# A state space layer on one core: when the experts' weights are loaded and split, and where its side work stands in the order of work

## The chip, the core and the metric

The kernel runs on one core of one Trainium2 chip. The core has TensorE (PE: matrix products, and transposes by a product with the identity), VectorE (DVE), ScalarE (ACT), GpSimd (POOL) and SyncE (SP, which here only issues transfers), 16 DMA engines, and two on-chip memories, SBUF and PSUM. Each engine takes its instructions in one order and waits, where it must, on semaphores that another engine or a transfer raises. The metric is the device time of one execution of the whole kernel in microseconds (us).

## The reference

The model has four layers: a state space layer, a layer of eight experts, a linear attention with a feed-forward part, and two local attention layers. The change touches only the first two, which the kernel computes together. On x of 4 x 1024 tokens of 256 values:

```python
x = x + _L0_attn_ref(_layernorm(x), ...)     # state space layer
x = x + _L0_ffn_ref(_layernorm(x), ...)      # experts
...
def _L0_attn_ref(x, W_in, conv_w, conv_b, W_xproj, W_dt, b_dt, A_log, D, W_out):
    xz = einsum('bld,ed->ble', x, W_in)
    u, z = split(xz, 2)                      # 512 channels each
    uc = silu(conv1d(u, conv_w, padding=1) + conv_b)     # 3 taps along the tokens
    dtp, Bm, Cm = split(uc @ W_xproj.T)      # 64, 16 and 16 wide
    dt = softplus(dtp @ W_dt.T + b_dt)
    A = -exp(A_log)                          # 16 states
    def step(h, inp):
        u_t, dt_t, B_t, C_t = inp
        h = exp(dt_t[:, None, :] * A[None, :, None]) * h + B_t[:, :, None] * u_t[:, None, :]
        return h, einsum('bn,bnh->bh', C_t, h)
    y = scan(step) + D * uc
    return x + (y * silu(z)) @ W_out.T

def _L0_ffn_ref(x, router_w, router_b, expert_w, expert_b):
    probs = softmax(x @ router_w.T + router_b)           # 8 experts
    top1, weights = argmax(probs), max(probs)
    y = (x @ expert_w[top1].T + expert_b[top1])
    return y * weights
```

## The kernel before

The method `mamba` computes both layers. Its 4096 tokens are cut into 16 sub-sequences `s` of 256 tokens, four to a batch row. The channels lie on the partitions (512 channels are four groups of 128), the tokens along them, and the 16 states are worked through one after the other. So there are 16 x 16 = 256 steps `k`, each one sub-sequence and one state `n`.

A step of the main loop does, in the order in which it is written:

- POOL keeps the last column of an earlier state (`keep`, tile `carry`), adds the carried start to the next one (`take`), and multiplies `uc` by a row of B for the step after the next: `product`, `hs<-uc,bn`, 128 x 1024, four `hs` buffers in all.
- ACT computes the decays exp(dt A) of half of the channels of the next step: `decays`, `da<-dt,a`, in PSUM, three buffers.
- DVE runs the recurrence in place over half of the channels, twice a step: `scan`, `hs<-da,hs`. "Scan 17" below means the second scan of step 8 of a sub-sequence, counted from 0.
- PE turns the result to tokens first, eight transposes: `tokens_first`, `ph<-ident,hs`, two `ph` buffers in PSUM. The step before's `ph` is weighted by C: for the states 0 to 5 by DVE into one sum (`acc<-ph,ct`), for the states 6 to 15 by ACT into tiles of their own (`term<-ph,ct`).

All else is side work, written as Python generators whose pieces end at `yield`:

- `features(s)`: loads a sub-sequence (`xr`), normalizes it (`st`, `mv`, `xn`), turns it (`xth`, `xtl`: a value split into a high and a low part, so that three products make one of higher precision).
- `channels(s)`: products with W_in (`pz`, `pu`), convolution and silu (`uc`, `sz`).
- `sizes(s)`: B, C and dt. `px` and `xd`; then B goes to DRAM (`bd`) and is read back to all partitions (`bn`); `ct`; two `pd` products, each with a group of ACT operations behind it; then a logarithm on ACT, which takes a table load on either side (`ACT_TABLE_LOAD`), and `dt`. With `first`, the next sub-sequence's decays can begin.
- `finish(s)`: sums the terms on PE (`py`), multiplies by the gate, the product with W_out (`po`), and adds it to `xr` on DVE (`xr<-xr,po`).
- `experts(s)`: norm, router (`pl`), choice (`cw`), bias (`pb`), and for every pair of experts six PE products into `pe`, weighted and added on DVE (`xr<-pe,cw,xr`, two of them); then `xr` is stored (`xs`).
- `expert_weights()`: runs once, in the first sub-sequence. It splits the router's weights `w_r` and the experts' weights `w_e`, eight parts of 128 x 512. For a part it loads `raw` (two buffers, shared by all of these loads and held until their splits are done), then ACT casts `raw` to `w_eh` and POOL subtracts, `w_el<-raw,w_eh`.

Where the pieces stand is given by lists of places. A step has three places (`PER`): 3k after the first scan and its output, 3k+1 after the second, 3k+2 after the transposes; a sub-sequence has 48, and a place below 0 or above 47 lies in the sub-sequence before or after. `side(place)` runs the next piece of each generator listed there, and within the loop every engine keeps the order in which its instructions were written (`nc.hold`); the order of transfers isn't held. `PSUM` tiles of all side work share three buffers (`tag="w"`), so a piece also waits for the piece three tiles earlier to be read.

All instructions are recorded in one helper (line 98), so that profile rows are told apart by their tiles. In the prologue, before the loop, `features(0)`, `features(1)`, `channels(0)`, `sizes(0)` and `features(2)` are run whole, then the first two `bn` loads are issued, and the loop is entered with two products and two decays. For sub-sequence 0 `sizes` does its `dt` sums on DVE instead of POOL (`dt<-dt,e`).

Of the kernel before, what the change touches and what calls it, by code (L numbers as in the profile page):

```python
# [17 lines left out]
P = 128  # L18
D = 256
# [15 lines left out]
NE = 8  # L35
# [38 lines left out]
def parts(width):  # L74
    return [slice(o, min(o + 512, width)) for o in range(0, width, 512)]


def run(steps):

    while True:  # L80
        try:
            next(steps)
        except StopIteration as end:
            return end.value
# [40 lines left out]
class Kernel:  # L125
# [145 lines left out]
    def mamba(self, xs):  # L271

        tc, ins = self.tc, self.ins
        nc = self.nc
# [4 lines left out]
        with ExitStack() as es:  # L279
            def pool(name, bufs, **kw):  # L280
                return es.enter_context(tc.tile_pool(name=name, bufs=bufs, **kw))

            early = pool("m_a", 1)
# [23 lines left out]
            for at in parts(2 * CH):  # L307
                for k in range(2):
                    raw = self.raw(early, ins["w_in"][k * P : (k + 1) * P, at])
# [20 lines left out]
            def expert_weights():  # L330
                w_e = Split(
                    wp.tile([P, 2, NE * D], F32R, name="w_eh"),
                    wp.tile([P, 2, NE * D], F32R, name="w_el"),
                )
                w_r = Split(
                    wp.tile([P, 2, NE], F32R, name="w_rh"), wp.tile([P, 2, NE], F32R, name="w_rl")
                )
                for k in range(2):
                    raw = self.raw(early, ins["w_r"][k * P : (k + 1) * P, :])
                    self.split(w_r[:, k, :], raw)  # L340
                yield
                for at in parts(NE * D):
                    for k in range(2):
                        raw = self.raw(early, ins["w_e"][k * P : (k + 1) * P, at])
                        self.split(w_e[:, k, at], raw, nc.gpsimd)
                        yield

                eb = wp.tile([2 * NE, 2, D], F32, name="eb")
                nc.gpsimd.memset(eb, 0.0)
                for t in range(2):  # L350
                    nc.scalar.dma_start(eb[t * NE : (t + 1) * NE, t, :], ins["e_b"])
                rank = wp.tile([P, NE], F32, name="rank")
                for e in range(NE):
                    nc.gpsimd.memset(rank[:, e : e + 1], float(NE - e))
                ew.update({"e": w_e, "r": w_r, "eb": eb, "rank": rank})
                ew["rb"] = self.row(wp, "router_b", NE)
                yield
# [51 lines left out]
            def channels(s):  # L409

                xt = st[s]["xt"]
                uc = mid.tile([P, NC, T], F32, name="uc", bufs=3)
                sz = mid.tile([P, NC, T], F32, name="sz", bufs=3)

                def gate(q):
                    pz = ps.tile([P, 2, T], F32, tag="w", name="pz")
                    for j in range(2):
                        o = CH + (2 * q + j) * P
                        self.mm3(
                            pz[:, j, :],  # L420
                            [(w_in[:, k, o : o + P], xt[:, k, 1 : T + 1]) for k in range(2)],
                        )
                    nc.scalar.copy(sz[:, 2 * q : 2 * q + 2, :], pz)

                def conv(c):
                    pu = ps.tile([P, T + 2], F32, tag="w", name="pu")
                    self.mm3(pu, [(w_in[:, k, c * P : (c + 1) * P], xt[:, k, :]) for k in range(2)])
                    nc.scalar.activation(
                        uc[:, c, :], pu[:, 1 : T + 1], AF.Identity,
                        bias=self.v("conv_b", c), scale=self.v("conv", NC + c),  # L430
                    )
                    return c, pu

                def neighbours(c, pu):
                    u = uc[:, c, :]
                    for j in (0, 2):
                        nc.vector.scalar_tensor_tensor(
                            u, pu[:, j : j + T], self.v("conv", j * NC + c), u, ALU.mult, ALU.add
                        )

                if s == 0:

                    for c in range(NC):
                        neighbours(*conv(c))
                    nc.scalar.activation(uc, uc, AF.Silu)
                    gate(0)
                    gate(1)
                    nc.scalar.activation(sz, sz, AF.Silu)
                else:
                    gate(0)  # L450
                    yield
                    gate(1)
                    one = conv(0)
                    yield
                    neighbours(*one)
                    one, two = conv(1), conv(2)
                    yield
                    neighbours(*one)
                    neighbours(*two)
                    one = conv(3)  # L460
                    yield
                    neighbours(*one)
                    yield

                    nc.scalar.activation(uc, uc, AF.Silu)
                    nc.scalar.activation(sz, sz, AF.Silu)
                st[s].update({"uc": uc, "sz": sz})
                yield
# [76 lines left out]
            def taken(s, o):  # L545

                first, at = st[s]["first"], slice(o, o + NS // 2)
                nc.gpsimd.tensor_tensor(
                    first[:, at, :], first[:, at, :], st[s - 1]["carry"][:, at, :], ALU.mult
                )  # L550
# [61 lines left out]
            def output(k, t):  # L612

                s, n = divmod(k, NS)
                ph, w = st[s]["ph", n, t], st[s]["ct"][:, t, n : n + 1]
                if n == 0 and t == 0:
                    st[s]["terms"] = [mid.tile([P, 2, CH], F32, name="acc", bufs=2)]
                terms = st[s]["terms"]
                acc = terms[0][:, t, :]
                if n in LATER:  # L620
                    if t == 0:
                        terms.append(mid.tile([P, 2, CH], F32, name=f"term{n}"))
                    nc.scalar.activation(terms[-1][:, t, :], ph, AF.Copy, scale=w)
                elif n == 0:
                    nc.vector.tensor_scalar(acc, ph, w, None, ALU.mult)
                else:
                    nc.vector.scalar_tensor_tensor(acc, ph, w, acc, ALU.mult, ALU.add)
# [35 lines left out]
            def experts(s):  # L663
# [83 lines left out]

            TAKEN = (19,)  # L750
            FINISH = (4, 7, 7, 13, 15, 17, 22, 25)
            CHANNELS = (-9, -5, -2, 0, 5, 8)
            SIZES = (10, 13, 16, 22, 26, 31, 37)
            FEATURES = (4, 14, 26, 30, 33, 34, 40)
            EXPERTS = (
                33, 33, 37, 40, 42, 43, 47, 51, 53, 53, 58, 62, 66, 75, 77, 81,
                82, 85, 87, 89, 95,
            )
            PER = 3
            plan = [[] for _ in range(PER * NSUB * NS)]  # L760

# [3 lines left out]
            def at(steps, step, places, plan=plan):  # L765
                for i in places:
                    plan[max(0, PER * step * NS + i)].append(steps)

            rest = []
            at(expert_weights(), 0, [PER * i + 1 for i in range(10)])  # L770
            for s in range(NSUB):
                last = s == NSUB - 1
                if s % SEQ:
                    at(iter([lambda s=s: taken(s, NS // 2)]), s, TAKEN)
                if s > 0:
                    at(finish(s - 1), s, FINISH)
                if not last:
                    at(channels(s + 1), s, CHANNELS)
                    at(sizes(s + 1), s, SIZES)
                if s + 3 < NSUB:  # L780
                    at(features(s + 3), s, FEATURES)
                if s > 0:
                    e = experts(s - 1)
                    if last:
                        at(e, s, [PER * i + 1 for i in range(9, NS) for _ in range(2)], later)
                        rest.append(e)
                    elif s + 1 == NSUB - 1:
                        at(e, s, EXPERTS[:7], later)
                        at(e, s + 1, [PER * i + 1 for i in range(14)], later)
                    else:  # L790
# [2 lines left out]
            run(features(0))  # L793
            run(features(1))
            run(channels(0))
            run(sizes(0))
            run(features(2))
            inputs(0)
# [13 lines left out]
            for k in range(K):  # L812
# [12 lines left out]
                if k:  # L825
                    output(k - 1, 0)
                side(PER * k)
                scan(k, 1)
# [1192 lines left out]
```

## Time and profile before

| what | us |
|---|---|
| median of the runs (3356.81 to 3365.26) | 3365.12 |
| the profiled execution's own time | 3363.27 |
| its span | 3361.6 |
| PE busy in the span | 3117.1 |
| DVE busy | 2558.7 |
| ACT busy | 2078.3 |
| POOL busy | 1932.1 |

The mean TensorE clock granted over the span was 0.963 of full speed. The span starts with a prologue up to the first scan at 43.80; the sub-sequences follow up to about 1084, then linear attention and the local attention layers. Times of rows are from the span's start. In a row of instructions the columns are the start, the duration, the engine, the line, the operation, the tile written and the tiles read, their shapes and the count; in square brackets is the engine's idle time before it, and what it waited for. A row of several instructions ("x3") tells the time from the first's start to the last's end. The page's shares are averages over stages with different limits: what bounds the first third isn't to be read from the whole.

### The profile page before, as it was taken

Reading aid. Unit: us, or ns where it says so; the run is one execution under the profiler, and the core shown is the slowest. Engines: PE = TensorE matmul, PEld = TensorE weight load, DVE = VectorE, ACT = ScalarE, POOL = GpSimd, SP = SyncE. Lnnn points to the kernel's source line nnn. Section 1 sums busy time; section 2 is a strip of 40 time slices with the busy share of each in tenths; the row PEclk is TensorE's granted clock in tenths of the full one; section 3 lists DMA queues with packets and bytes.
Section 4 is the critical chain, followed back from the end, with each engine's and each line's share of the span. In section 5 each row is a group of like instructions: output and inputs, shape, how many; then the busy total and the mean of one; then the engine's idle time right before and its main releaser. Section 6 shows DMA issues by size and latency. Waiting matters only on the chain.

```text
span 3361.6 us, 60088 instructions
## 1 busy us (share of the span) xinstructions
PE 3117.1 (93%) x22000; PEld 2670.1 (79%) x22000; DVE 2558.7 (76%) x5684; ACT 2078.3 (62%) x4194; POOL 1932.1 (57%) x2285
## 2 busy tenths in 40 slices
PE   5788899898888899999999999899999999999998
PEld 4677777777777688888888888688888888888886
DVE  6799999999997766666776757677777677767763
ACT  7888887888884323443434343666666776667664
POOL 5988988898885401101110114766677766767671
PEclk7799999999998999999999999899999999999998
DMA  2011111111110300000000011201111111111111
GB/s 93 32 45 39 39 51 39 39 39 45 36 41 30 99 8 4 14 7 14 20 10 10 20 39 50 79 26 43 45 51 50 51 47 55 43 47 39 46 35 35
DMA packets 83974, 130.62 MB, mean 39 GB/s; under 512 B 10080, under 2 KB 58016, under 8 KB 83680
## 3 DMA queue, kind: packets, MB, share of 16 engines
q1 hardware_dynamic: 81216, 124.68, 11.6%
q8 instruction: 175, 2.87, 0.4%
q10 hardware_dynamic: 2320, 1.57, 0.2%
q14 instruction: 119, 0.97, 0.1%
q0 software_dynamic: 144, 0.52, 0.0%
HBM read 99.21 MB, written 27.53 MB: 38 GB/s over the span
## 4 chain that ended last, share of the span: by engine, by line
PE 58%; DVE 18%; ACT 12%; POOL 6%; issue 4%; DMA 2%; POOLq 0%; SPq 0%; ACTq 0%; DVEq 0%
PE pw L98 10%; PE pq L98 10%; PE po L98 8%; PE pa L98 7%; DVE hs L98 7%; PE pt L98 7%; ACT L98 3%; PE pf L98 3%; PE pp L98 3%; PE pv L98 2%; ACT gl L98 2%; DVE acc L98 2%; POOL hs L98 2%; PE pe L98 2%; PE ph L98 2%
## 5 line engine op out<-in xcount | busy, mean ns | idle before, releaser
L98 DVE TENSOR_TENSOR_SCAN hs<-da,hs 128x512 f32<-128x512 f32 x512 | 609.2, 1209 | 20.9 <-ACT da L98 10.8
L98 POOL TENSOR_TENSOR hs<-uc,bn 128x1024 f32<-128x1024 f32 x256 | 608.7, 2378 | 26.8 <-PE ph L98 22.5
L98 PE MATMUL ph<-ident,hs 128*128 128x128 f32 x2048 | 333.8, 299 | 126.8 <-ACT term L98 52.0
L98 PEld LDWEIGHTS ph<-ident,hs 128*128 128x128 f32 x2048 | 249.8, 152 | 208.5 <-DVE hs L98 71.8
L98 ACT ACTIVATE da<-dt,a 128x510 f32<-128x510 f32 x512 | 342.8, 686 | 91.9 <-DVE hs L98 85.2
L98 POOL MEMSET va<- 128x8 f32 x64 | 7.3, 117 | 575.2 <-PE pk L98 458.2
L98 POOL TENSOR_TENSOR u<-u,ro 128x512 f32<-128x512 f32 x128 | 175.5, 1371 | 246.9 <-DVE ro L98 201.2
L98 ACT ACTIVATE sm<-sm,mx 128x256 f32<-128x256 f32 (+1 forms) x512 | 248.5, 488 | 97.8 <-DVE mx L98 96.8
L98 PE MATMUL pq<-wqkvh,yt 128*128 128x512 f32 x768 | 287.8, 416 | 0.7 <-ACT yt L98 0.7
L98 POOL TENSOR_SCALAR sm<-sm,sums 128x256 f32<-128x256 f32 (+1 forms) x512 | 237.2, 481 | 83.0 <-DVE sums L98 77.7
L98 ACT ACTIVATE term<-ph,ct 128x512 f32<-128x512 f32 x320 | 207.6, 681 | 45.1 <-PE ph L98 45.0
L98 ACT ACT_TABLE_LOAD x146 | 187.3, 1283 | 59.7 <-DVE gl L98 31.9
L98 DVE CUSTOM_DVE_ANT_0 sm<-pp,band 128x256 f32<-128x256 f32 (+1 forms) x512 | 177.8, 403 | 42.5 <-PE pp L98 42.1
L98 POOL TENSOR_TENSOR ss<-ss,power 128x16 f32<-128x16 f32 x64 | 187.7, 2932 | 5.3
L98 ACT ACTIVATE e<-pq 128x512 f32<-128x512 f32 x128 | 75.9, 597 | 182.7 <-PE pq L98 170.1
L98 PEld LDWEIGHTS pq<-wqkvh,yt 128*128 128x128 f32 x768 | 144.9, 189 | 38.3 <-issue 9.8
L98 ACT ACTIVATE sq<-pq 128x512 f32<-128x512 f32 x128 | 76.6, 599 | 142.8 <-DVE ro L98 106.6
L98 PE MATMUL py<-ident,term 128*128 128x128 f32 x1280 | 159.5, 276 | 0.0
L98 PE MATMUL pq<-wqkvl,yt 128*128 128x512 f32 x384 | 152.4, 397 | 0.0
L98 PE MATMUL pa<-fh,w1h 128*128 128x512 f32 x320 | 134.2, 420 | 19.1 <-ACT v L98 15.7
L98 PEld LDWEIGHTS py<-ident,term 128*128 128x128 f32 x1280 | 147.1, 144 | 0.1
L98 PE MATMUL po<-va,am 128*128 128x65 f32 x1024 | 146.4, 260 | 0.0
(323 smaller groups left out, 10256.3 us busy)
## 6 DMA issues: line engine op xcount, KB each, us to landing
bn<-bd SPq DMA_DIRECT2D x64, 512.0 KB
tab<-tab SPq DMA_DIRECT2D x64, 128.0 KB
line<-yg SPq DMA_DIRECT2D x64, 128.0 KB
hn<-line SPq DMA_DIRECT2D x64, 128.0 KB
xr<-in_x SPq DMA_DIRECT2D x16, 256.0 KB
xs<-xr SPq DMA_DIRECT2D x16, 256.0 KB
hn<-xs SPq DMA_DIRECT2D x16, 256.0 KB
ls<-hn SPq DMA_DIRECT2D x16, 256.0 KB
```

What stands on the lines that cost most here:

```text
L98: now = f(*args, **kw)
```

## The change

Two things are changed in `mamba`. `expert_weights()` is started by hand in the prologue, between `channels(0)` and `sizes(0)`: there it splits `w_r` and issues the loads of the first two parts of `w_e`. Each later piece splits one part, and then issues the load of the part after the next. Its pieces have a list of places of their own, `WEIGHTS`: three at place 1, then 4, 7, 10, 13, 17 and 25, where before there were ten at 1, 4, 7 and so on up to 28. And all the other lists of places are replaced. The same operations are done as before.

```diff
                 for k in range(2):
                     raw = self.raw(early, ins["w_r"][k * P : (k + 1) * P, :])
                     self.split(w_r[:, k, :], raw)
-                yield
-                for at in parts(NE * D):
-                    for k in range(2):
-                        raw = self.raw(early, ins["w_e"][k * P : (k + 1) * P, at])
-                        self.split(w_e[:, k, at], raw, nc.gpsimd)
-                        yield
+
+                order = [(k, at) for at in parts(NE * D) for k in range(2)]
+                raws = [self.raw(early, ins["w_e"][k * P : (k + 1) * P, at]) for k, at in order[:2]]
+                yield
+                for i, (k, at) in enumerate(order):
+                    self.split(w_e[:, k, at], raws[i], nc.gpsimd)
+                    if i + 2 < len(order):
+                        k, at = order[i + 2]
+                        raws.append(self.raw(early, ins["w_e"][k * P : (k + 1) * P, at]))
+                    yield
...
-            TAKEN = (19,)
-            FINISH = (4, 7, 7, 13, 15, 17, 22, 25)
-            CHANNELS = (-9, -5, -2, 0, 5, 8)
-            SIZES = (10, 13, 16, 22, 26, 31, 37)
-            FEATURES = (4, 14, 26, 30, 33, 34, 40)
+            TAKEN = (20,)
+            FINISH = (4, 7, 7, 10, 14, 17, 21, 25)
+            CHANNELS = (-11, -5, -2, 1, 6, 9)
+            SIZES = (10, 13, 18, 22, 25, 31, 43)
+            FEATURES = (7, 11, 25, 30, 33, 34, 38)
             EXPERTS = (
-                33, 33, 37, 40, 42, 43, 47, 51, 53, 53, 58, 62, 66, 75, 77, 81,
-                82, 85, 87, 89, 95,
+                32, 35, 37, 39, 41, 44, 47, 52, 53, 53, 58, 62, 67, 75, 78, 80,
+                82, 84, 87, 88, 91,
             )
+            WEIGHTS = (1, 1, 1, 4, 7, 10, 13, 17, 25)
...
-            at(expert_weights(), 0, [PER * i + 1 for i in range(10)])
+            ew_parts = expert_weights()
+            at(ew_parts, 0, WEIGHTS)
...
             run(channels(0))
+            next(ew_parts)
             run(sizes(0))
```

## The prediction

> **What bounds the kernel now.** I read the page first, then busy time per stretch, then the waits of VectorE (DVE) in one stretch, then TensorE (PE) in stretches as long as one step of its clock.
>
> ```profile
> PE 3117.1 (93%) x22000; PEld 2670.1 (79%) x22000; DVE 2558.7 (76%) x5684; ACT 2078.3 (62%) x4194; POOL 1932.1 (57%) x2285
> PE 58%; DVE 18%; ACT 12%; POOL 6%; issue 4%; DMA 2%; POOLq 0%; SPq 0%; ACTq 0%; DVEq 0%
> ```
>
> PE leads on the average, but the change touches only `mamba`, the first 1090 us or so. Busy time per stretch (length, then the engines, granted clock, DMA share, GB/s) shows another order there:
>
> ```profile
> 43.80:109.00 65.20, 42.57 (x179) 30.30 (x180) 50.03 (x61) 54.56 (x92) 49.36 (x59) 0.63 0.17 58
> 369.00:434.00 65.00, 58.03 (x374) 49.15 (x372) 62.20 (x92) 53.32 (x92) 57.33 (x72) 0.95 0.12 42
> 954.00:1019.00 65.00, 56.02 (x337) 47.08 (x336) 60.69 (x84) 50.62 (x87) 56.98 (x67) 0.90 0.13 45
> ```
>
> DVE (third) is busy 62.20 of 65.00 in a steady stretch, PE only 58.03. The first sub-sequence, 43.80 to 109.00, has ACT at 54.56 and no engine full: a chain, not an engine, sets it. `xr<-xr,po` comes once in a sub-sequence: 404.20, 469.13, 534.04, 598.90, 663.77, so the period is 64.86 us. What DVE waits for in such a stretch:
>
> ```profile
> DVE xr L98 <- PE po L98: 1.7, 1, 1.7
> DVE xr L98 <- PE pe L98: 0.5, 1, 0.5
> ```
>
> That is all: 2.1 to 2.2 us, so without waits the period would be 64.86 - 2.1 = 62.75. Both waits are for PE, and the next view says why (PE is the first column, its clock the sixth):
>
> ```profile
> 394.82:398.24 3.42, 1.79 (x11) 1.12 (x11) 3.42 (x5) 3.39 (x6) 2.66 (x4) 1.00 0.00 0
> 398.24:401.65 3.41, 3.41 (x11) 2.68 (x10) 3.41 (x5) 2.45 (x5) 3.35 (x2) 0.51 0.00 0
> 401.65:405.06 3.41, 3.41 (x24) 3.16 (x23) 1.71 (x3) 3.01 (x4) 3.15 (x8) 0.99 0.02 5
> 405.06:408.48 3.42, 1.37 (x6) 0.76 (x5) 3.35 (x6) 3.38 (x5) 3.42 (x4) 1.00 0.29 110
> 408.48:411.89 3.41, 2.97 (x11) 2.76 (x12) 3.41 (x4) 3.41 (x7) 3.33 (x7) 0.51 0.12 43
> 411.89:415.30 3.41, 3.41 (x22) 2.93 (x21) 2.84 (x8) 3.41 (x7) 3.41 (x2) 0.99 0.00 0
> ```
>
> In stretches of 3.41 us the granted clock is either full or half: half after a stretch with PE busy 1.79 or 1.37, full after a busier one. At half clock eight `po` matmuls take 3.31 us instead of 1.89, and eight `ph` with six `pe` 3.90 (408.92 to 412.82) instead of 2.44 (404.00 to 406.44). The period, 64.86, is 19.0 such stretches: each period meets the clock at the same point, and its length is held by that.
>
> **Part 1, the experts' weights.** Two rows of the start matter, and two of the first step:
>
> ```profile
> 32.66 10.66 POOL L98 TENSOR_TENSOR hs<-uc,bn 128x1024 f32<-128x1024 f32 x4
> 36.23 7.65 DVE L98 TENSOR_TENSOR dt<-dt,e 128x512 f32<-128x512 f32 x3
> 55.15 0.62 ACT L98 CAST w_eh<-raw 128x512 fp32r<-128x512 f32 x1 [1.61 <-DMA raw<-in_w_e]
> 55.84 1.26 POOL L98 TENSOR_TENSOR w_el<-raw,w_eh 128x512 fp32r<-128x512 f32 x1 [12.52 <-ACT w_eh L98]
> ```
>
> Added ahead of `sizes(0)`: the two `w_r` splits, ACT casts of 0.14 each and DVE subtractions of 0.14 to 0.16. DVE had 0.48 idle there, so +0.1 to +0.5; I take +0.2. On SP's queue the two `w_r` and two `w_e` loads now stand before the `bd` store; the second `w_e` load waits for a buffer until about 18, and `bd` was issued only at 24.72, so it costs nothing; if the split slipped past 24.72, the prologue would slip with it.
>
> POOL's order changes: before, it ran `product(0)` to `product(3)` back to back (32.66 to 43.32), then sat idle 12.52. After, three `w_el` subtractions stand between `product(2)` and `product(3)`. The last of the three `dt` operations took 2.83 us (41.05 to 43.88) beside a POOL product of 2.79 (40.54 to 43.33); the same form alone took 0.69 (`w_inl<-raw,w_inh`). With POOL not multiplying then, the first decay on ACT (43.91) starts 2.83 - 0.7 = 2.1 earlier. The bounds are 0 (something else keeps them apart) and 2.1; I take 2.0.
>
> Against that, three splits stand at place 1. The third needs a load that can be issued only when POOL's first `w_el` has freed a buffer; before, issue to landing of such a load took 3.55 (51.58 to 55.13). ACT then holds at the third cast, about 4.1 us, with `uc` and a decay queued behind it; `product(3)` stands behind the third `w_el` on POOL. Walked through with rows of before, scan 2 comes 0.95 later and scan 3 1.85 later; from step 4 on the parts that before did at places 13 to 28 are already done, and by the sub-sequence's end, where before had DVE idles of 1.1 to 3.8 us in 87 to 109 for decays and products, the walk is 1.0 (by ACT) to 1.3 (by POOL) ahead. I take -1.1, bounds -3 (the stall hidden) and +3 (most of it kept). Start and first sub-sequence: +0.2 - 2.0 - 1.1 = -2.9, bounds -5 and +3.
>
> **Part 2, the places.** No engine gets more or less work, so the floor stays 62.75; only order moves. Four moves are of consequence in a steady sub-sequence (time from its first scan, 366.88 in the stretch above):
>
> - `SIZES` 16 to 18: the second `pd` now stands behind the transposes of step 5, which wait for DVE's 12th accumulation, at 25.8. `pd` runs by 26.5 and its ACT group starts at 27.64, where before it started at 26.22 (393.10): +1.4. From that group through the table loads and Ln to the decay of scan 20, before took 13.12 without its 1.35 wait for `ph`; one 0.61 pass fewer stands in between, so 12.51. The decay starts at 40.15 (before 40.69). But DVE now comes sooner.
> - `po` after more PE work (`pd`, `pe`): PE stays busy ahead of it, no half-clock stretch falls on it, and it ends at about 35.6, when DVE is there. The 1.70 wait goes. What is late next: `xr<-po` 0.6, scan 18 1.1, two `pe` additions 0.9, scan 19 1.1, so DVE wants scan 20 at 39.4, and the decay ends at 40.8: a new wait of 1.4 for ACT.
> - `EXPERTS` 77, 81, 82 to 78, 80, 82: scan 20 and 21 stand ahead of a `pe` addition that was behind scan 19. The wait on that `pe` is met later by DVE, but one more scan (1.12) stands behind it: 20.07 to the period's end instead of 18.95.
> - The PE gap ahead of the transposes of step 9 grows from 2.48 (406.44 to 408.92) to about 3.5 (38.0 to 41.5), since `pe` is done earlier and `ph` still waits for ACT's term. Some 3.41 stretch always has at least half of it, so half clock follows once a period: `pe` at 41.5 + 3.94 = 45.44, and the period 45.44 + 20.07 = 65.5; at full clock throughout, 1.4 less, 64.1.
>
> Between 64.1 and 65.5 lies 64.85, nineteen stretches of 3.413. A period that is shorter meets the half-clock stretch a little further on each time, and is delayed more, until it holds: as before. So I take 64.85, no change in sub-sequences 3 to 12. Settling there from a start that is 2.9 earlier costs between nothing and 3.4, one stretch; I take +1.5. In the two last sub-sequences without features (62.9 to 63.0 before) the new wait of scan 20 is partly kept: +0.5, bounds -1 and +2.
>
> The moves of `TAKEN`, `FINISH`, `CHANNELS` and `FEATURES` cost nothing by themselves: `py` (13 to 10, 15 to 14, 22 to 21) and `pz` (-9 to -11) run in PE's 7 us of idle time a period. On SP's queue a period keeps its order (store of `xs`, load of `xr`, `bn`, `bd`, three `bn`); the load of `xr` was issued at 368.74, and its statistics on DVE come after scan 7, at about 383, instead of at 388: 14 us for a transfer whose nearest row took 3.55. If that cover went, DVE would wait there; a late `pz` would show as an ACT wait of about 1 (`sz<-pz` had 1.06).
>
> Sum: -2.9 + 1.5 + 0.5 = -0.9 against the profiled execution's 3363.27: 3362.4. The median of the runs, 3365.12, stands 1.85 above that execution, so 3364.2, told as 3364.
>
> [...]
>
> **The rivals.**
>
> *The period comes free of the clock, faster.* If the gap before step 9 is 1 us shorter than I walked, no half-clock stretch falls on the path, and the period is 64.1 or, with the wait of scan 20 gone too, 62.75. For it: that wait rests on a chain of some twenty rows, good to about 1 us; DVE's 1.70 for `po` does go. Against: ACT's term is on the same chain. 0.75 x 11 = 8.3 to 2.1 x 11 = 23, with -2.9 and +0.5: 3342 to 3354, middle 3351.
>
> *The ACT chain sets the period, slower.* `pd` behind step 5 is a fixed 1.4; if the `ph` ahead of it or `pd` itself falls into half clock (`ph` 1.97 instead of 1.04), scan 20 waits 0.9 more, the period lies between 65.0 and 66.4 and can't hold at 64.85. It decides from 0.75 us on. At 65.7 it is 0.85 x 11 = +9, with 66.4 +17; if the start gains nothing and the tail keeps 2: 3365 + 9 + 2 = 3376, up to 3382. For it: the new wait has nothing behind it to hide in. Against: PE was at full clock at 390 in the trace.
>
> *Nothing to hide.* The `w_e` loads were idle POOL time of 12.52 that nobody waited for; if the stall of 4.1 on ACT stays, the start gives +3 instead of -2.9, 3370 with the period unchanged.
>
> **How the numbers follow.** Chances: period held at 64.85, 0.43, 3364, own range 3360 to 3369; faster 0.28; ACT chain 0.24; the stall kept 0.05. A difference of 0.3%, 10 us, is about what a measurement can tell from none. Of the faster rival 0.25 lies below 3355; of the slower two 0.26 lies above 3375 (the stall together with a longer period among it), which leaves 0.49 between. With a tenth left out on each side, 3346 to 3380.
>
> **What would show it.** Right: first decay at about 41.9 instead of 43.9, ACT stalled about 4 us at its third `w_eh`, `product(3)` behind it; no DVE wait for `po`; a wait of about 1.4 for a decay at scan 20; one half-clock stretch a period instead of two; `xr<-po` 64.85 apart. Wrong: another distance. Below 64.5, the clock doesn't hold the period; above 65.2, look at what ACT's `pd` group waits for. I would also be wrong if a move that I cost at nothing, `xr` or `pz`, shows a wait of its own in DVE or ACT.

## The result: slower, by about 27 us

The changed kernel takes 3390.24 us (median of four, 3387.32 to 3396.98) against 3363.2 (3356.81 to 3365.26): 27.0 more. The record's ratio is 1.0097, 95% interval 1.0082 to 1.0113; the two medians divide to 1.0080. The profiled execution took 3390.77, its span is 3389.1. The forecast of 3364, range 3346 to 3380, was wrong; the rival that named the ACT chain had the direction and the place, and was still too small.

The page's busy times and chain, after:

```profile
PE 3150.1 (93%) x22000; PEld 2694.9 (80%) x22000; DVE 2559.0 (76%) x5684; ACT 2075.6 (61%) x4194; POOL 1932.0 (57%) x2285
PE 58%; DVE 20%; ACT 13%; POOL 4%; issue 4%; DMA 1%; POOLq 0%; ACTq 0%; DVEq 0%
```

The same 22000 PE instructions took 33 us longer, while DVE and POOL did not change and ACT fell by 2.7: PE's clock was lower (0.950 over the span for 0.963). Laid side by side by the same instruction, the two traces differ by -1.45 us at the first scan (42.35 against 43.80), -3.1 at sub-sequence 1, and from there the loss grows by about 2.3 a sub-sequence to +28.9 at the last one's first scan (1040.39 against 1011.54). Within the last one it shrinks to +23.5 (last scan 1101.80 against 1078.34); behind `mamba` it stays near +27 to the end. The first scans of sub-sequences 5 to 12 come at 373.62, 441.14, 508.09, 574.82, 642.29, 709.52, 776.29 and 843.78: a period of 67.2 on the average where before it was 64.86.

What DVE waits for in one such period, 574.8 to 642.3, and busy time in the first and in that one (length, PE, PEld, DVE, ACT, POOL, granted clock, DMA share, GB/s):

```profile
DVE hs L98 <- ACT da L98: 2.5, 2, 1.4
DVE xr L98 <- PE pe L98: 1.9, 1, 1.9
DVE xr L98 <- PE po L98: 0.2, 1, 0.2
```

```profile
42.35:108.64 66.29, 41.80 (x210) 31.01 (x210) 52.09 (x61) 57.78 (x98) 54.38 (x64) 0.72 0.17 56
574.82:642.29 67.47, 60.31 (x372) 50.87 (x372) 62.27 (x92) 52.92 (x91) 55.24 (x61) 0.90 0.13 41
```

DVE's work is as before (62.27); it waits 4.6 where it waited 2.1. The wait for `po` went, as forecast; scans now wait 2.5 for decays (1.4 and 1.1) and `xr` 1.9 for `pe`. In stretches of the clock:

```profile
593.02:596.43 3.41, 2.61 (x17) 1.83 (x15) 3.38 (x7) 2.90 (x9) 3.33 (x4) 1.00 0.02 5
596.43:599.84 3.41, 2.56 (x12) 1.48 (x12) 3.41 (x5) 3.38 (x7) 3.33 (x3) 1.00 0.10 38
599.84:603.26 3.42, 3.22 (x10) 2.17 (x10) 3.42 (x6) 0.87 (x2) 2.56 (x3) 0.50 0.36 115
603.26:606.67 3.41, 3.41 (x10) 2.25 (x9) 3.24 (x4) 2.80 (x7) 2.40 (x3) 0.50 0.00 0
606.67:610.08 3.41, 3.41 (x23) 2.89 (x23) 2.18 (x3) 3.41 (x6) 2.33 (x2) 1.00 0.00 0
613.50:616.91 3.41, 0.88 (x4) 0.38 (x2) 2.45 (x4) 3.37 (x4) 3.33 (x3) 1.00 0.08 29
616.91:620.32 3.41, 2.67 (x11) 2.48 (x12) 3.19 (x4) 3.41 (x7) 3.41 (x3) 0.50 0.33 125
```

Two half-clock stretches, 599.84 to 606.67, are new. They follow a stretch in which PE was busy 2.56 of 3.41; before, between 300 and 900 us, the busiest that half clock followed had 1.79. The one ahead of it, busy 2.61, was followed by full clock. The first of the two is itself busy 3.22, and half clock follows it again. So busy time alone doesn't tell what comes next. With the two behind 616.91 a period of this kind has four half-clock stretches, where before had two. What PE and ACT did there, in order of time:

```profile
597.73 1.13 PE L98 MATMUL pb<-eb,cwt 16*128 16x256 f32 x4
599.00 0.41 PE L98 MATMUL ph<-ident,hs 128*128 128x128 f32 x2 [0.15 <-DVE acc L98]
600.04 1.76 PE L98 MATMUL ph<-ident,hs 128*128 128x128 f32 x6 [0.63 <-DVE hs L98]
601.73 2.07 PE L98 MATMUL pd<-xd,w_dt 64*128 64x256 f32 x4
```

```profile
603.84 0.47 ACT L98 ACTIVATE e<-pd,vecs 128x256 f32<-128x256 f32 x1 [3.13 <-PE pd L98]
607.90 1.22 DVE L98 TENSOR_TENSOR_SCAN hs<-da,hs 128x512 f32<-128x512 f32 x1 [1.40 <-ACT da L98]
612.63 1.28 ACT L98 ACT_TABLE_LOAD   x1
616.30 0.69 ACT L98 ACTIVATE da<-dt,a 128x510 f32<-128x510 f32 x1
617.09 1.22 DVE L98 TENSOR_TENSOR_SCAN hs<-da,hs 128x512 f32<-128x512 f32 x1 [1.10 <-ACT da L98]
617.65 1.97 PE L98 MATMUL ph<-ident,hs 128*128 128x128 f32 x8 [3.27 <-ACT term L98]
622.21 1.00 DVE L98 SCALAR_TENSOR_TENSOR xr<-pe,cw,xr 128x256 f32<-128x256 f32 x2 [1.87 <-PE pe L98]
```

`pd` stands behind the transposes of step 5, as walked, but both run at half clock (`pd` 2.07; 1.13 at full). ACT idles 3.13, its group starts 29.0 into the sub-sequence (603.84 - 574.82) instead of 27.64. The next decay stands behind that group, and scan 15 waits 1.40 for it (607.90). The decay of scan 20 comes at 41.5 instead of 40.15, and the transposes behind the gap fall into the next half-clock stretch (1.97 for eight), on which `pe` and then DVE wait.

### The profile page after: what moved, and what is told of

Same layout as the page of the kernel before. It is cut to its first block, busy times and chain, and to the rows that moved or that the text cites. A ratio compares the mean times of both kernels' runs of the same rounds, so it can differ in the third digit from the quotient of the medians.

```text
span 3389.1 us, 60109 instructions
## 1 busy us (share of the span) xinstructions
PE 3150.1 (93%) x22000; PEld 2694.9 (80%) x22000; DVE 2559.0 (76%) x5684; ACT 2075.6 (61%) x4194; POOL 1932.0 (57%) x2285
## 4 chain that ended last, share of the span: by engine, by line
PE 58%; DVE 20%; ACT 13%; POOL 4%; issue 4%; DMA 1%; POOLq 0%; ACTq 0%; DVEq 0%
PE pw L98 10%; PE pq L98 10%; DVE hs L98 8%; PE pa L98 7%; PE po L98 7%; PE pt L98 7%; PE pf L98 3%; PE pp L98 3%; DVE acc L98 3%; ACT L98 2%; PE pv L98 2%; ACT da L98 2%; PE ph L98 2%; PE pe L98 2%; ACT gl L98 2%
## 5 line engine op out<-in xcount | busy, mean ns | idle before, releaser
L98 PE MATMUL ph<-ident,hs 128*128 128x128 f32 x2048 | 346.2, 308 | 114.3 <-ACT term L98 56.8
L98 PEld LDWEIGHTS ph<-ident,hs 128*128 128x128 f32 x2048 | 262.8, 157 | 197.3 <-ACT term L98 78.7
L98 DVE SCALAR_TENSOR_TENSOR xr<-pe,cw,xr 128x256 f32<-128x256 f32 x256 | 121.6, 475 | 33.6 <-PE pe L98 29.1
```

The costliest lines, as they stand in the source:

```text
L98: now = f(*args, **kw)
```

## The experiments

Theory A: the one number in `SIZES` is the cause, through the order and through the clock. Theory B: the moved additions of the experts are. Three questions followed: does half clock at `pd` go with the rows that `pb` contracts over (A1) or with PE's busy time alone (A2), do the half-clock stretches (A) or DVE's own work (C) hold the period, and what are the other parts worth.

| kernel | median | ratio to before, 95% interval | period | half-clock stretches, 300 to 900 us |
|---|---|---|---|---|
| before | 3360.9 | | 64.88 | 18 |
| after | 3390.2 | 1.0097 (1.0082 to 1.0113) | 67.17 | 35 |
| `e1_pd_back` | 3369.8 | 1.0026 (1.0016 to 1.0036) | 64.86 | 37 |
| `e2_pd_alone` | 3379.1 | 1.0056 (1.0041 to 1.0071) | 65.55 | 28 |
| `e3_pb_rows` | 3372.1 | 1.0044 (1.0025 to 1.0062) | 65.64 | 24 |
| `e4_weights_alone` | 3365.6 | 1.0015 (1.0004 to 1.0026) | 64.87 | 15 |
| `e5_pd_pb` | 3354.1 | 0.9970 (0.9956 to 0.9984) | 64.33 | 14 |
| `e6_weights_spaced` | 3365.8 | 1.0007 (0.9991 to 1.0023) | 64.88 | 15 |
| `e7_pe_twice` | 3354.9 | 0.9979 (0.9967 to 0.9991) | 63.16 | 2 |
| `e8_pd_pb_pe` | 3356.3 | 0.9984 (0.9968 to 1.0001) | 63.29 | 8 |
| `e9_places_less_pd` | 3368.5 | 1.0019 (1.0008 to 1.0031) | 64.90 | 34 |
| `e10_places_pb` | 3355.3 | 0.9980 (0.9970 to 0.9989) | 64.33 | 15 |
| `e11_pe_twice_to_13` | 3345.3 | 0.9948 (0.9933 to 0.9964) | 63.11 | 0 |

Before's median is that beside `e1` to `e4` (20 executions, 3351.98 to 3368.1); the ratio of after is to its own four. The ratios of `e5` to `e8` are to 31 executions of before (median 3360.7), those of `e9` to `e11` to 19 (3361.1). Periods are mean distances of the first scans of sub-sequences 5 to 12 of the profiled execution (for `e4` and `e6` the usual one, since in three of theirs, with one half-clock stretch fewer, the period fell to 63.2 to 64.4; for `e8` that of sub-sequences 1 to 10). Before settles at 64.86 from sub-sequence 8 on. The last column counts, among some 175 stretches of 3.413 us, those with half of the clock granted. `e1` and `e9` have about as many of them as the changed kernel, with the period of before: what they cost depends on where they fall. The profiled execution of `e1` (3362.48) was the fastest of its ten, so its row shows less than its median has.

**`pd` back in the changed kernel.**

```diff
-            SIZES = (10, 13, 18, 22, 25, 31, 43)
+            SIZES = (10, 13, 16, 22, 25, 31, 43)
```

> The changed kernel with one number put back: the second pd group at place 16 instead of 18. Theory A (that move is the cause: pd stands behind the transposes of step 5, and the PE stretch left with ph and pb alone is followed by half clock, which slows those transposes and pd as well): the half-clock stretches around pd vanish, the ACT group behind it starts at about 26.2 instead of 29.0 us into the sub-sequence, the period falls from 67.1 to 64.9 or less, and the time from 3390 to 3360 to 3367. Theory B (the experts' additions moved behind scans 20 and 21 are the cause): the wait of xr for pe and the wait of scan 20 stay at over 3 us together, the period stays above 66 and the time above 3378.

The period fell to 64.86 and the time to 3369.8, 20.5 under the changed kernel. The place is the cause of most of the loss, and theory B, as the main cause, is out; the time stayed 3 above A's range, so other parts cost something too. DVE waits 2.0 in a period:

```profile
DVE xr L98 <- PE pe L98: 1.4, 1, 1.4
DVE hs L98 <- ACT da L98: 0.3, 1, 0.3
DVE xr L98 <- PE po L98: 0.3, 1, 0.3
```

One thing was not as expected: half clock at `pd` stayed.

```profile
585.28:588.69 3.41, 2.44 (x12) 1.49 (x12) 3.41 (x4) 3.38 (x9) 3.25 (x5) 1.00 0.00 0
588.69:592.10 3.41, 3.41 (x12) 2.52 (x12) 3.41 (x5) 2.56 (x7) 2.34 (x2) 0.50 0.47 154
590.85 0.47 ACT L98 ACTIVATE e<-pd,vecs 128x256 f32<-128x256 f32 x1 [0.85 <-PE pd L98]
```

So with the other new places half clock falls on `pd` even at place 16, and the number 18 isn't alone in bringing it. It does little harm there: `pd` runs directly behind `pb`, and its ACT group starts 26.1 into the sub-sequence (590.85 - 564.77), as before (26.2). The period is nineteen stretches of the clock once more, with quite other waits than before.

**`pd` moved in the kernel before.**

```diff
-            SIZES = (10, 13, 16, 22, 26, 31, 37)
+            SIZES = (10, 13, 18, 22, 26, 31, 37)
```

> The kernel before with that one number changed: the second pd group at place 18 instead of 16. Theory A: the period rises from 64.86 to between 66 and 67.5, with half clock at pd, and the time to 3378 to 3395. Theory B: the period stays within 0.5 of 64.86, the time at 3358 to 3371.

3379.1, in A's range: this number alone costs 18.3, and with before's other places too it brings half clock at `pd` in most periods. The period rose less than expected in the profiled execution, 64.5 to 66.4, 65.55 on average, and in part the loss is of the first sub-sequences (70.87 for the first instead of 67.92).

**`pb` over 128 rows in the changed kernel.** The tile of `cwt` and that of the biases get 128 rows, zeros below the sixteenth; `pb` contracts over all of them. Number and order of PE's instructions stay, and nearly their length (four `pb` take 1.03 instead of 1.13).

```diff
-                eb = wp.tile([2 * NE, 2, D], F32, name="eb")
+                eb = wp.tile([P, 2, D], F32, name="eb")
+                cwt = wp.tile([P, P], F32, name="cwt")
+                nc.gpsimd.memset(cwt, 0.0)
...
-                cwt = wk.tile([2 * NE, P], F32, name="cwt")
-                nc.scalar.copy(cwt, pt[0 : 2 * NE, :])
+                cwt = ew["cwt"]
+                nc.scalar.copy(cwt[0 : 2 * NE, :], pt[0 : 2 * NE, :])
```

> The changed kernel with its order untouched, but the small product pb contracts over 128 rows (112 of them zeros) instead of 16; the same number of instructions of the same length. It is a test of what the clock counts. If rows of the array in use count as activity (theory A1), the stretch with pb is busy enough, pd and the transposes ahead of it run at full clock, the ACT group behind pd starts 1.4 earlier, and the period falls to 64.9 to 66, the time to 3360 to 3376. If only time in use counts (A2), nothing changes: half clock stays at pd, period 67.1, time 3386 to 3394.

3372.1, 18 less than the changed kernel, in the range of A1. One stretch of this kernel with the same eight transposes and four `pb`, and the next:

```profile
523.50:526.91 3.41, 2.23 (x13) 1.47 (x12) 3.41 (x5) 3.38 (x8) 3.41 (x7) 1.00 0.00 0
526.91:530.32 3.41, 2.34 (x12) 1.29 (x10) 3.41 (x5) 1.69 (x4) 3.41 (x5) 1.00 0.42 154
```

Busy 2.23, and full clock follows; with 16 rows, busy 2.56 was followed by half. Between 300 and 900 us all ten stretches in which a `pb` of 128 rows begins are followed by full clock, two of them at half clock themselves; all twelve of the changed kernel, with 16 rows, by half, five of them at half clock themselves. (One more stretch of `e3` holds only the last 0.2 us of a `pb`, and half clock follows it.) So PE's busy time alone didn't tell which clock came next; with `pb` over 128 rows instead of 16 it was full instead of half. Why, no run shows.

The ACT group now starts at 27.62 (530.12 - 502.50), where the walk of the prediction had 27.64:

```profile
530.12 0.47 ACT L98 ACTIVATE e<-pd,vecs 128x256 f32<-128x256 f32 x1 [1.72 <-PE pd L98]
```

With full clock at `pd` and the order of the changed kernel the period is 65.64: of the 2.3 that it lost, the clock there made 1.5 and the order 0.8. So the order as walked doesn't settle at 64.85 either.

**The weights' part alone**, with the places of before.

```diff
-            at(expert_weights(), 0, [PER * i + 1 for i in range(10)])
+            ew_parts = expert_weights()
+            at(ew_parts, 0, WEIGHTS)
...
             run(channels(0))
+            next(ew_parts)
             run(sizes(0))
```

> The kernel before with only the experts' weights moved (loads two parts ahead, their own places), all other places as before. By the prediction's first part: first scan at about 41.9 to 42.4, first sub-sequence 1 to 2 us shorter, the period 64.86 as before, the time 1 to 5 us under that of before, within what can be measured: 3358 to 3365. If the stall at the third cast is kept: 2 to 5 us over, 3365 to 3370.

3365.6, 4.8 over before: the second case. The first scan came at 42.90, 0.9 earlier, the last `dt` operation took 0.68 instead of 2.83, but ACT stalled 4.01 and 1.51 for `raw`, and the first sub-sequence took 69.52, 1.6 more. So at sub-sequence 1 this part alone stands 0.7 behind before, not ahead.

**The weights' pieces one step apart.**

```diff
-            WEIGHTS = (1, 1, 1, 4, 7, 10, 13, 17, 25)
+            WEIGHTS = (1, 4, 7, 10, 13, 16, 19, 22, 25)
```

> The kernel before with the weights' part alone, but with its pieces one step apart (places 1, 4, 7, 10 and on to 25) instead of three at place 1. If the stall of ACT at the third cast (4.0 us) is what that part costs: no stall over 1.5, first sub-sequence 66 to 67.5 instead of 69.5, the time 2 to 5 under that with three at place 1 (3365.6). If that part costs by the settling of the period alone: the same time within 2.

A miss: the stall went, but the first sub-sequence took 69.21 all the same. DVE then waited 10.0 for products of POOL (8.0 in `e4`, 7.1 before); that the splits on POOL delay them is argued, not tested. The medians, 3365.8 and 3365.6, don't tell the two apart; at sub-sequence 2 this one stands 0.8 ahead of before, the other 2.2 behind.

**`pd` back and `pb` over 128 rows** (both edits above on the changed kernel).

> The changed kernel with the second pd group back at place 16 and pb over 128 rows. With pd back alone the period stood at 64.85, with two half-clock stretches after a stretch with PE at 0.72, and one after the gap ahead of the transposes of step 9. Theory A (the clock holds the period): the stretches around pd go to full clock, the ACT chain comes about 1 earlier, the gap shortens, the period falls below 64.5, to 62.5 to 64.3, and the time 6 to 25 under that with pd back alone (3369.8): 3345 to 3364. Theory C (DVE's own work holds it): the period stays at 64.85 and the time within 4 of 3369.8.

3354.1, 15.7 under `pd` back alone, and under the kernel before. All eleven stretches in which a `pb` begins are followed by full clock, all nine of `e1`, with 16 rows, by half; the twenty are at full clock themselves. That is as A has it: with 14 half-clock stretches instead of 37 the period fell below 64.86, to 63.28 in the middle sub-sequence without any, though to 64.33 on average, just above what was expected, as half clock still comes behind the gap ahead of step 9.

Four kernels now have the new places, with `pd` at 16 or 18 and `pb` over 16 or 128 rows. The place costs 20.5 with 16 rows (after less `e1`) and 18.0 with 128 (`e3` less `e5`); the few rows cost 18.1 at 18 and 15.7 at 16. The two causes nearly add: `pd` behind the transposes of step 5 is late by itself (its ACT group 27.62 into the sub-sequence in `e3`, 26.2 before), and half clock there makes it later (29.0 in the changed kernel). `pb` over 128 rows with the places of before wasn't run.

**The first two experts' products twice over, on the kernel before.**

```diff
-                        self.mm3(
-                            pe.rearrange("p j d -> p (j d)"),
-                            [...],
-                        )
+                        for _ in range(2 if e == 0 else 1):
+                            self.mm3(
+                                pe.rearrange("p j d -> p (j d)"),
+                                [...],
+                            )
```

> The kernel before with the products of the first two experts done twice over (12 matmuls more in a sub-sequence, the second pass writes the same result again; one pe in the stretch ahead of po, one ahead of the gap before the transposes of step 9). Theory A (PE's idle time brings half clock, and half clock holds the period at 64.86): more work makes it faster: no half clock around po, the wait for po under 0.5, the period 62.8 to 63.8, the time 10 to 25 under before. Theory C (the two waits are there whatever the clock): no change, or slower by the 2.8 us of added PE work per period, 3361 to 3390.

The period fell to 63.16, and the last scan came at 1054.02 instead of 1078.34, 24.3 earlier, though PE had more to do. But the time fell only by 5.9, below what A expected (10 to 25): the rest was given back behind the last scan. PE is busy 113.60 of 120 us from 1120 on (before), the experts of the last sub-sequences and the next layer's first products are left, and the doubled products lie in it too. `e8_pd_pb_pe`, with the same doubling on `e5`:

> The changed kernel with pd back at place 16, pb over 128 rows, and the products of the first two experts done twice. Theory A: no half clock in the part from pd to step 10, the period 61.5 to 63.5, the time 3335 to 3352, under the kernel before. Theory C: as with pd back and pb alone, or slower by the added work.

3356.3, above A's range: the period is 63.29 up to sub-sequence 10, as A says, then 64.86 with half clock at `pd`; the last scan came at 1059.38, and again most of it was given back. So the doubling was left out of the last two sub-sequences:

```diff
-                        for _ in range(2 if e == 0 else 1):
+                        for _ in range(2 if e == 0 and s < NSUB - 2 else 1):
```

> The kernel before with the products of the first two experts done twice, but not in the last two sub-sequences, whose experts run when the scans are done. With all of them doubled the last scan came 24 earlier (1054.0 against 1078.3) and the end only 8. If the doubled work itself fills PE at the hand-over: the last scan stays at 1053 to 1056 and the time falls by 4 to 6 to 3349 to 3351. If the gain is lost because PE has work of its own there that the scans had covered: the time stays within 2 of 3354.9.

3345.3, 0.52% under before (interval 0.36 to 0.67%), and 9.6 under `e7`: more than the 4 to 6 of the doubled work, and outside both ranges. The last scan came at 1058.15, 20.2 earlier (later than the 1053 to 1056 expected), and the end 18.0 earlier. What else than the doubled work was given back in `e7` is open. One period of it, the same of before, and all DVE waits of two of its periods:

```profile
554.27:617.20 62.93, 57.89 (x384) 48.80 (x385) 62.06 (x93) 52.82 (x91) 55.22 (x58) 1.00 0.13 43
```

```profile
561.59:626.45 64.86, 57.91 (x372) 49.05 (x373) 62.13 (x92) 53.22 (x92) 55.90 (x61) 0.95 0.13 42
```

```profile
DVE hs L98 <- ACT da L98: 0.5, 2, 0.2
```

Twelve instructions more, the same busy time, the clock at 1.00, and no wait for `po` or `pe`: both waits of the kernel before (3.4 for `po` and 0.8 for `pe` in two periods) went with the half clock.

**The new places without `pd` and without the weights' part** (both undone as in `e1` and `e4`), and the same with `pb` over 128 rows.

> All the new places except that of the second pd group (16, as before), with the experts' weights done as before the change. With the new weights part the same places gave 3369.8 (8.9 over the kernel before), and that part alone 4.8 over. If the parts add: 3363 to 3367, ratio 1.000 to 1.002, period 64.85. If the weights part is what cost there: 3360. If the other places cost all of it: 3368 to 3372.

> The same places, weights as before the change, and pb over 128 rows: what was 3354.05 with the new weights part. If that part costs 4.8 here too: 3347 to 3352. If it costs nothing: 3352 to 3357. The period 63.2 to 64.7 in both cases.

3368.5 and 3355.3. Beside `e1` and `e5`, which have the weights' part, that is 1.3 less and 1.2 more: that part costs nothing that can be told in this company. The remaining places cost 7.4; 18.3 for `pd` and these make 25.7 of the 27 to 29 lost. With `pb` over 128 rows the same places are 5.8 under before, so the clock has a part in the 7.4. Where they lie is open: the profiled execution of `e9` has a span 1.5 shorter than before's, and its time (3361.84) is among the lowest of ten that reach 3372.

## Why the prediction was wrong, step by step

- **What bounds the kernel**: right. The period was held at nineteen stretches of 3.413 by half-clock stretches: with 2 and 0 of them instead of 18, `e7` and `e11` have 63.16 and 63.11 for 64.88. 62.75 as the floor is near the 62.93 of `e11`.
- **Weights, start**: right. The first decay came at 41.55 (41.9 expected), the last `dt` took 0.68, the `w_r` splits cost 0.4 (0.2 taken, 0.1 to 0.5 as bounds), the third cast stalled 3.99 (4.1). The first scan lies between 42.09 and 43.08 in the seven kernels with this part, between 43.80 and 44.72 in the six without: 1.7 earlier on the mean, for 1.8.
- **Weights, first sub-sequence**: -1.1 was expected. Start and first sub-sequence together gave -3.1 in the changed kernel, beside -2.9, but that is in part luck: with the places of before the same part makes the first sub-sequence 1.6 longer (`e4`), and with the new places and `pd` back it takes 69.08 (`e1`), not the 66.29 of the changed kernel. The rival of the stall (3370) is near `e4` in the time, but not by its cause: `e6` took the stall away and stayed at 3365.8.
- **`po`**: right. Its wait fell to between 0.2 and 0.9.
- **`SIZES` 16 to 18**: the step that failed. The transposes of step 5 and `pd` were priced at full clock. I had read the clock by busy time, and PE's stretches there were well filled. Before, `pd` and `pb` stood in one stretch (388.06, busy 3.41, full clock behind it); in the new order (the first `pd` products 19.3 into the sub-sequence for 20.5, the second at 18) a stretch with `pb` has eight transposes and four products of 16 rows, and half clock followed it (twelve of twelve). `pd` began 0.4 later than the 26.5 that I gave and took 2.07 instead of 1.13, its ACT group came 1.4 later, and the decay of scan 20 1.3 later. The late group also made scan 15 wait 1.4 for its decay, a wait that the walk didn't have. With full clock at `pd` the walk holds: 27.62 for 27.64 in `e3`. This mis-pricing is worth 1.5 a period, 18.1 in the time (after less `e3`).
- **"So I take 64.85"**: the second step that failed. It put a later `pd` at no cost, as the clock would hold any period between 64.1 and 65.5; that was my estimate from the one period of before. In the changed kernel the period had become 67.2. But `e3`, at full clock there, doesn't hold at 64.85 either: its periods run from 65.0 to 66.1, and it is 11.3 over before. Why nothing holds it there is open. Of the walk's other waits, scan 20 had 1.1 for 1.4, the gap 3.27 for 3.5, and the wait for `pe` behind scan 21 was 1.1 to 1.9. One half-clock stretch a period was forecast; most periods had four.
- **The rival of the ACT chain** named just this ("if the `ph` ahead of it or `pd` itself falls into half clock") and put 65.0 to 66.4 and 3382 at most; it got 0.24, because "PE was at full clock at 390 in the trace". That row was of the order before, and the new order changed which products shared a stretch. The rival also counted one slowed group at scan 20; there was the wait of scan 15 too, and two half-clock stretches ahead of step 9 came on top.
- **The last sub-sequences**: priced +0.5, measured +1.4 and +2.4 (64.39 for 63.01, 65.00 for 62.63). They have the same `pd`.
- **Moves priced at nothing**: DVE never waited for `xr` or ACT long for `pz` (0.9), as said; but `e9` shows 7.4 in medians that the steps don't explain.
- **A sum**: the faster rival's lower end, 3342, leaves out its own -2.9 + 0.5; with them it is 3340. Nothing else rests on it.

## What to carry to other kernels

Where PE isn't the bound but others wait for it, look at its granted clock in stretches of its own length (3.41 us here), and at what each stretch holds, before a small product is moved: here half clock followed the stretches with `pb` over 16 rows, at full clock busy 2.34 to 2.56, and full clock those with `pb` over 128 rows, busy 2.23 to 2.37. A loop whose period is a whole number of such stretches, as before was (64.86, nineteen of 3.413), may be held by the clock, and small gains elsewhere may then vanish in it. Cheap products at places with slack, done twice with the same result, can be worth more than their time: 12 more beside 372 per period made this kernel 0.52% faster.

## What the runs showed of the hardware that was not expected

- The rows that `pb` contracts over went with the clock of the next stretch: those busy 2.34 to 2.56 of 3.41 us with `pb` over 16 rows were followed by half clock, those busy 2.23 to 2.37 with `pb` over 128 rows by full clock. With those at half clock themselves it is twelve of twelve (after) and ten of ten (`e3`), and nine of nine (`e1`) and eleven of eleven (`e5`) with `pd` back.
- Half clock came after stretches in which PE was busier than in any that it followed in the kernel before: 2.34 to 2.56 of 3.41 us at full clock in the changed kernel, at most 1.79 before (300 to 900 us). Other stretches of the changed kernel, busy 2.49 to 2.52 at full clock, were followed by full clock.
- Work added to PE made the program faster (`e7`, `e11`): 63.1 to 63.2 a period with 384 PE instructions against 64.86 with 372.
- The changed kernel's periods repeat in threes from sub-sequence 7 on, 66.7, 67.5 and 67.2: three last 201.47 us, which is 59.0 stretches of 3.413. Whether the clock held that period too, at another number, no run tests.
- Time gained in `mamba` isn't all kept: 24.3 at its last scan became 8.4 at the end of `e7`'s profiled execution, 20.2 became 18.0 where the last two sub-sequences weren't burdened.
